# Layer 0's scores in runs of nine over a seven-bank PSUM ring, with exponentials of 1, 1, 3, 2 and 2 banks

## The chip, the cores and the metric

The kernel runs on one NeuronCore of a Trainium2 chip. The metric is the device time of one execution in microseconds, the median of several runs. The profile is one further execution with the hardware profiler on. In the text TensorE (PE) is the matrix engine, with its weight loads shown apart (PEld), ScalarE (ACT) the activation engine, VectorE (DVE) the elementwise engine, POOL the general-purpose engine, SP the engine that only issues DMAs. PSUM, the memory into which TensorE writes[...].

## The reference

Two layers are applied to x (2 images, 256 channels, 64x64 pixels). Layer 0, the only one that the change touches, is a group normalisation, then attention with 8 heads of 32 channels over all 4096 pixels, added to x:

```python
qkv = jnp.einsum('bchw,oc->bohw', x, qkv_w) + qkv_b[None, :, None, None]
...
attn_logits = jnp.einsum('bhci,bhcj->bhij', q, k) * scale
attn_weights = jax.nn.softmax(attn_logits, axis=-1)
out = jnp.einsum('bhij,bhcj->bhci', attn_weights, v)
```

Layer 1 (1x1 convolutions, two attentions within small groups of pixels, a 3x3 convolution) works on the result, and the kernel computes it after layer 0 for each image in turn.

## The kernel before

For each of the two images the kernel makes queries, keys and values (`project0`), then runs layer 0's attention (`attention0`, from L464), then layer 1.

**The tiling of the attention.** The queries of a head are cut into 2 groups of 4 tiles of 512, so an image has 16 groups (g), and the keys into 32 blocks (j) of 128. A *unit* is one key block against one query tile: its score matmul (L505) takes 128 keys as weights (128x128) and 512 queries as the moving data, and fills one PSUM bank. ScalarE takes the exponential of one to three banks with one instruction (L511), without subtracting a maximum, and writes it to `es` in SBUF. A block of four units is then multiplied with its values (`quarters`, L521): the weights are 128x32, the four query tiles lie side by side in the array's four column quarters, and everything of a group adds up in one further bank, `av`. These are fp32 matmuls, each of which the trace shows as two. `work_of` (L570) cuts a block into two halves of 256 columns, save the first and last block of a group; such a half, 8 matmuls in the trace, is a *step*. A group has 62 steps, an image 992.

**The sum of the exponentials** (the softmax's denominator) is made by VectorE (`add_rows`, L558), which adds blocks up elementwise in `added`, and for seven of the 32 blocks by DMAs from POOL's queue that accumulate in SBUF (L566, L568). Once a group is over, `finish` (L592) lets TensorE add the 128 partitions up with a matrix of ones (`sum_rows`), ScalarE copies the result (L598), and after some DMAs and a reciprocal VectorE scales the group's output. The row sum needs a PSUM bank for a short while.

**The rounds.** Seven PSUM banks hold scores, as three tiles: `sa` of three banks, `sb` and `sc` of two. `scores` (L491) fills the three in turn and puts one exponential behind each: a round of seven units. The exponentials go to a ring of 28 places in SBUF (`RING`, L452; 17 in `es`, 11 elsewhere, so `at_places` cuts a group there); `places` holds the place of each unit. In a round in which a row sum (or a small matmul for layer 1's statistics) is due, `sa` takes two units only, and its third bank is lent out (`spare`); this happens 15 times an image for row sums and twice for statistics.

**The order of the work** is written by hand for TensorE, ScalarE and VectorE (`tc.manual_schedule`, L771): their instructions are queued in the order in which the code issues them. The loop from L779 issues a round of scores with its exponentials and then steps of the work on older units: those whose exponentials were issued in earlier rounds (`have`, taken before the round). `share` paces the steps to the units, `must` makes sure that what lies in places about to be overwritten has been used, and a round is broken off where a group ends. What is due with a lent bank stands in `wanted` and is called (`use`) after two steps. The tile framework adds the semaphore waits[...].

The lines that matter below: L500 (the tiles `sa`, `sb`, `sc`), L505 (score matmul), L511 (exponential), L521 (value matmuls and row sums), L598 (copy of a row sum), L762 (copy of a group's `av` bank), L737 (the bank for the last group's row sums), L779 to L804 (the loop).

Of the kernel before, what the change touches and what calls it, by code (L numbers as in the profile page):

```python
# [9 lines left out]
F32 = mybir.dt.float32  # L10
I32 = mybir.dt.int32
F32R = mybir.dt.float32r
AF = mybir.ActivationFunctionType
# [4 lines left out]
P = 128  # L18
B, C, H, W = 2, 256, 64, 64
N = H * W  # L20
T = 512
# [4 lines left out]
NH0 = C // HD0  # L26
# [14 lines left out]
def direct_layers(ctx: ExitStack, tc: tile.TileContext, a: dict, out: bass.AP, bad: bass.AP):  # L41
# [3 lines left out]
    nc = tc.nc  # L45
# [11 lines left out]
    psum = {}  # L57

    def w4(shape, name, dtype=F32):
        return work.tile(shape, dtype, tag="w4", name=name)  # L60
# [304 lines left out]
    SC0 = 1.0 / math.sqrt(HD0)  # L365
# [8 lines left out]
    NJ = N // P  # L374
# [77 lines left out]
    RING, RING_A = 28, 17  # L452
# [11 lines left out]
    def attention0(b, xts, held):  # L464
# [10 lines left out]
        n_units = NH0 * 2 * NJ * 4  # L475
# [4 lines left out]
        places = []  # L480
        n_places = 0

        def at_places(first, n):

            while n > 0:
                at = first % RING
                m = min(n, (RING_A if at < RING_A else RING) - at)
                yield m, es[:, at : at + m, :] if at < RING_A else held["es"][:, at - RING_A : at - RING_A + m, :]
                first, n = first + m, n - m

        def scores(spare):  # L491

            nonlocal n_places
            bank = None
            for tag, size in (("sa", 3), ("sb", 2), ("sc", 2)):
                first = len(places)
                n = min(size - (spare and size == 3), n_units - first)
                if n <= 0:
                    break
                sc = psum["sc"].tile([P, size, T], F32, tag=tag, name=f"{tag}_{b}_{first}")  # L500
                if spare and size == 3:
                    bank = sc[:, size - 1, :]
                for i in range(n):
                    g, (j, u) = (first + i) // (4 * NJ), divmod((first + i) % (4 * NJ), 4)
                    nc.tensor.matmul(  # L505
                        sc[:, i, :], held["k", g // 2][:, j * P : (j + 1) * P], held["q", g, u // 2][:, u % 2, :],
                        start=True, stop=True,
                    )
                i = 0
                for m, dst in at_places(n_places, n):  # L510
                    nc.scalar.activation(dst, sc[:, i : i + m, :], AF.Exp, scale=SC0)  # L511
                    i += m
                places.extend(range(n_places, n_places + n))
                n_places += size
            return bank

        def quarters(dst, lhs, rhs, start, stop, part=None):

# [17 lines left out]
        def add_rows(g, j):  # L536
            if j == 0:
                sums[g] = psum["sc"].tile([P, T], F32, tag="av", name=f"av_{b}_{g}")
                added[g] = [w4([P, 2, T], f"e_{b}_{g}_{w}") for w in range(2)]
                return  # L540
            for w in range(2):
                dst = added[g][w]
                if j in summed(g):
                    if w == 0:
                        add_in_memory(g, j)
                    continue
                if j == 1:
                    first = two_units(g, 0, w), two_units(g, 1, w)
                    if len(first[0]) == len(first[1]) == 1:
                        nc.vector.tensor_add(dst, first[0][0][1], first[1][0][1])  # L550
                    else:
                        for s in range(2):
                            nc.vector.tensor_add(dst[:, s, :], unit(g, 0, 2 * w + s), unit(g, 1, 2 * w + s))
                    continue
                for s, src in two_units(g, j, w):
                    if g == last and j in SUMMED_LAST:
                        continue
                    nc.vector.tensor_add(dst[:, s, :], dst[:, s, :], src)  # L558
# [11 lines left out]
        def work_of(g, j):  # L570


            if (g, j) < (last, NJ - 3):
                add_rows(g, j)
            for part in (None,) if j in (0, NJ - 1) else range(2):
                if part == 1:
                    yield
                quarters(
                    sums[g], held["v"][:, (g // 2) % 2, j, :], lambda u: unit(g, j, u), j == 0, j == NJ - 1, part
                )  # L580

        def sum_rows(g, rows):
            if g == last:
                for part in range(2):
                    for j in SUMMED_LAST:
                        quarters(rows, ones, lambda u: unit(g, j, u), j == SUMMED_LAST[0], False, part)
                    quarters(rows, ones, lambda u: acc[u], False, False, part)
                    quarters(rows, ones, lambda u: added[g][u // 2][:, u % 2, :], False, True, part)
                return
            quarters(rows, ones, lambda u: added[g][u // 2][:, u % 2, :], True, True)  # L590
# [140 lines left out]
        def steps():  # L731

            for done in range(NH0 * 2 * NJ):
                g, j = divmod(done, NJ)
                if (g, j) == (last, NJ - 3):
                    assert len(places) == n_units
                    held["rows"] = psum["sc"].tile([P, 3, T], F32, tag="sa", name=f"rows_{b}")[:, 2, :]  # L737
                    for i in (NJ - 3, NJ - 2, NJ - 1):
                        add_rows(g, i)
                    sum_rows(g, held["rows"])  # L740
                for _ in work_of(g, j):
                    yield done
                if g and j == 0:

                    for w in range(2):
                        dst = added[g - 1][w]
                        for s in range(2) if w == 0 else (slice(0, 2),):
                            nc.vector.tensor_add(dst[:, s, :], dst[:, s, :], acc[s] if w == 0 else pair)
                    waiting.clear()
                if g and j == 1:  # L750
                    wanted.append(late[0].send)
                if g and j in (9, 17):
                    next(late[0])
                for what in also.get((g, j), ()):
                    what()
                if j == 4 and g % 2 == 0 and g // 2 + 1 < NH0:
                    fetch_head(b, g // 2 + 1, held)
                if j == NJ - 1:
                    waiting.append(g)
                    avs = w4([P, 2, T], f"avs_{b}_{g}")  # L760
                    if g < last:
                        nc.scalar.copy(avs[:, 0, :], sums[g])  # L762
                    copied[g] = avs
                    late[:] = [finish(g)]
                    next(late[0])
                    if g + 2 < NH0 * 2:
                        fetch_queries(b, g + 2, held)
                yield done + 1

        E = mybir.EngineType  # L770
        with tc.manual_schedule(engines={E.PE, E.Activation, E.DVE}):  # L771

            per_group = 2 * NJ - 2
            work, begun, taken = steps(), 0, 0
            scores(False)
            final = False
            while not final:  # L779
                have = len(places)  # L780
                use = wanted.pop(0) if wanted else None
                bank = scores(use is not None)
                final = have == n_units
                ready = have // 4
                share = have * per_group // (4 * NJ) - 2

                must = sum(place < n_places + 7 - RING for place in places[: 4 * ready : 4])
                if must % NJ == 1:
                    must += 1
                assert must <= ready  # L790
                here = 0
                while begun < ready and (taken < share or begun < must or final or use is not None):
                    if use is not None and here == 2:
                        use(bank)
                        use = None
                        continue
                    here += 1
                    group = begun // NJ
                    begun = next(work)
                    taken += 1  # L800
                    if begun // NJ > group and begun >= must and not final and use is None:
                        break
                if use is not None:
                    use(bank)  # L804
            assert next(work, None) is None
            return *finish_last(last), st
# [585 lines left out]
    for b in range(B):  # L1392
        xts = x_first if b == 0 else ahead["xts"]
        w0 = w0_first if b == 0 else ahead["w0"]
        with tc.tile_pool(name=f"ps0_{b}", bufs=8, space=PSUM) as psum["ps"]:
# [7 lines left out]
            held = project0(b, xn, w0)  # L1403
# [571 lines left out]
```

## Time and profile before

| what | value |
|---|---|
| time, median of 3 runs | 3115.34 us (3115.27 to 3119.38) |
| span of the profiled execution | 3116.4 us |
| TensorE busy in the span | 3031.2 us (97%) |
| VectorE busy | 2467.0 us (79%) |
| ScalarE busy | 2313.6 us (74%) |
| layer 0's attention, first image | 118 to 1158 us of the span |
| layer 0's attention, second image | 1664 to 2710 us |
| score matmuls (L505) | 4096: 1736 in `sa`, 1180 each in `sb` and `sc` |
| value matmuls into `av` (L521) | 15872 |
| exponentials (L511) | 1770: 590 for each of the three tiles |
| copies of row sums (L598), of `av` (L762) | 30 each, 585 and 607 ns |

The profiled execution's span differs from the median of the runs by 1.1 us. A profile line of the timeline gives the start in us, the length in us, the engine, the line of the kernel, the operation, the tiles written and read, their shapes and the count; in brackets stands the idle time of the engine before it and what ended that. `v` as the output of an exponential is the second part of the ring. The page's slices cut the span into 40 parts and give each engine's busy share in tenths. The granted TensorE clock is 1.00 of full speed throughout the attention.

### The profile page before, as it was taken

How to read it: one execution, taken by the hardware profiler on the slowest of the kernel's cores; microseconds unless marked ns; L12 is line 12 of the kernel's file. 1: busy time of each engine (PE TensorE's matmuls, PEld its weight loads, DVE VectorE, ACT ScalarE, POOL GpSimd, SP SyncE). 2: the span in 40 equal slices, each digit the busy share in tenths (PEclk: the TensorE clock that was granted, in tenths of full speed). 3: DMA queues.
4: the chain of work that ended last, by engine and by line, in shares of the span. 5: the costliest groups of instructions: out<-in, count | busy, mean ns of one | idle time of the engine just before them, and what ended most of it. 6: DMA issues, size and time to landing. Idle time of an engine off the chain costs nothing. (4 is left out here: it accounts for less than half of the span.)

```text
span 3116.4 us, 62659 instructions
## 1 busy us (share of the span) xinstructions
PE 3031.2 (97%) x25129; PEld 1830.6 (59%) x25129; DVE 2467.0 (79%) x3126; ACT 2313.6 (74%) x2436; POOL 836.7 (27%) x923
## 2 busy tenths in 40 slices
PE   6999999999999999999989999999999999999998
PEld 4555555555555556677755555555555555476765
DVE  4599989999899999856556998989989999834543
ACT  2699999999999984622237999999999999734333
POOL 2022222222222231055301222222222222305440
PEclk9999999999999999999999999999999999999999
DMA  7969679797897761230159687796888975700000
GB/s 241 270 132 185 143 150 172 154 178 150 164 181 154 145 133 33 75 134 29 41 193 268 128 176 151 156 176 138 177 162 164 181 153 123 170 4 4 21 14 22
DMA packets 243787, 424.41 MB, mean 136 GB/s; under 512 B 99112, under 2 KB 109916, under 8 KB 241308
## 3 DMA queue, kind: packets, MB, share of 16 engines
q0 software_dynamic: 94992, 238.36, 39.8%
q1 hardware_dynamic: 147580, 181.68, 21.6%
q8 instruction: 199, 3.26, 0.4%
q14 instruction: 104, 0.85, 0.1%
q10 hardware_dynamic: 912, 0.27, 0.0%
HBM read 119.03 MB, written 68.39 MB: 60 GB/s over the span
## 5 line engine op out<-in xcount | busy, mean ns | idle before, releaser
L558 DVE TENSOR_TENSOR e<-e,es 128x1024 f32<-128x1024 f32 (+1 forms) x956 | 1038.6, 1142 | 79.6 <-ACT es L511 77.9
L521 PE MATMUL av<-es,v 128*32 128x256 f32 (+1 forms) x9644 | 746.7, 390 | 0.0
L558 DVE TENSOR_TENSOR e<-e,v 128x1024 f32<-128x1024 f32 (+1 forms) x640 | 675.2, 1107 | 47.7 <-ACT v L511 46.6
L511 ACT ACTIVATE es<-sa 128x1536 f32<-128x1536 f32 (+1 forms) x444 | 635.7, 1432 | 93.1 <-PE sa L505 54.9
L505 PE MATMUL sa<-q,k 128*128 128x512 f32 x1736 | 561.4, 430 | 9.2 <-ACT avs L598 3.5
L521 PE MATMUL av<-v 128*32 128x256 f32 (+1 forms) x6228 | 506.5, 389 | 0.0
L521 PEld LDWEIGHTS av<-es,v 128*32 128x32 f32 x9644 | 316.1, 109 | 299.4 <-issue 160.6
L505 PEld LDWEIGHTS sa<-q,k 128*128 128x128 f32 x1736 | 280.0, 188 | 291.8 <-issue 135.4
L505 PE MATMUL sc<-q,k 128*128 128x512 f32 x1180 | 371.4, 396 | 1.7 <-ACT es L511 0.7
L505 PE MATMUL sb<-q,k 128*128 128x512 f32 x1180 | 371.0, 395 | 1.1 <-ACT es L511 1.1
L521 PEld LDWEIGHTS av<-v 128*32 128x32 f32 x6228 | 216.5, 109 | 178.6 <-issue 81.2
L511 ACT ACTIVATE es<-sc 128x1024 f32<-128x1024 f32 x296 | 306.9, 1037 | 0.0
L511 ACT ACTIVATE v<-sc 128x1024 f32<-128x1024 f32 x294 | 304.9, 1037 | 0.1
L511 ACT ACTIVATE es<-sb 128x1024 f32<-128x1024 f32 x296 | 302.0, 1020 | 3.8 <-DMA acc<-es 3.8
L511 ACT ACTIVATE v<-sb 128x1024 f32<-128x1024 f32 x294 | 300.0, 1020 | 0.0
L505 PEld LDWEIGHTS sb<-q,k 128*128 128x128 f32 x1180 | 221.2, 188 | 55.4 <-ACT es L511 2.9
L505 PEld LDWEIGHTS sc<-q,k 128*128 128x128 f32 x1180 | 210.5, 188 | 71.8 <-ACT es L511 12.1
L511 ACT ACTIVATE v<-sa 128x1536 f32<-128x1536 f32 (+1 forms) x146 | 209.2, 1433 | 35.6 <-PE sa L505 17.0
L948 PE MATMUL mm<-v,wf 128*128 128x256 f32 x1024 | 227.6, 380 | 1.5 <-DVE z L957 1.5
L568 POOL DMA_DIRECT2D es<-es x116 | 98.9, 853 | 475.6 <-ACT es L511 424.3
L948 PEld LDWEIGHTS mm<-v,wf 128*128 128x128 f32 x1024 | 193.3, 190 | 36.8 <-issue 9.9
L938 POOL TENSOR_TENSOR v<-col 128x512 f32<-128x512 f32 x128 | 165.1, 1316 | 179.2 <-ACT rk_sr L1089 39.2
(262 smaller groups left out, 3179.0 us busy)
## 6 DMA issues: line engine op xcount, KB each, us to landing
acc<-es POOLq DMA_DIRECT2D x128, 512.0 KB, 6.2
acc<-v POOLq DMA_DIRECT2D x84, 512.0 KB, 6.4
es<-es POOLq DMA_DIRECT2D x136, 256.0 KB, 4.5
v<-es POOLq DMA_DIRECT2D x132, 256.0 KB, 5.1
k<-wk_halves SPq DMA_DIRECT2D x64, 512.0 KB
q<-wq_halves SPq DMA_DIRECT2D x256, 128.0 KB
v<-v POOLq DMA_DIRECT2D x90, 256.0 KB, 5.4
es<-v POOLq DMA_DIRECT2D x86, 256.0 KB, 3.9
```

The costliest lines, as they stand in the source:

```text
L505: nc.tensor.matmul(sc[:, i, :], held["k", g // 2][:, j * P : (j + 1) * P], held["q", g, u // 2][:, u % 2, :], start=True, stop=True,)
L511: nc.scalar.activation(dst, sc[:, i : i + m, :], AF.Exp, scale=SC0)
L521: nc.tensor.matmul(dst[HD0 * u : HD0 * u + HD0, n], lhs, rhs(u)[:, n], start=start, stop=stop)
L558: nc.vector.tensor_add(dst[:, s, :], dst[:, s, :], src)
L568: nc.gpsimd.dma_start(out=dst, in_=src, accum_op=ALU.add)
L938: (nc.gpsimd.tensor_add if plus else nc.gpsimd.tensor_sub)(dst, rows(one), rows(two))
L948: nc.tensor.matmul(mm[:, m, r, :], wf[:, k, 4 * r + q, m * P : (m + 1) * P], v[r // 2][:, r % 2, k, :], start=k == 0, stop=k == KC - 1,)
```

## The change

The three tiles become one tile of seven banks, `ring`, and a unit's bank is its place modulo 7. A run has nine units, in groups of 1, 1, 3, 2 and 2, each followed by its exponential; `runs_of` cuts a group where it would pass the last bank or the ring's two ends in SBUF. After each score matmul and each exponential, `tc.declare_no_dep` tells the framework that it doesn't depend on the exponentials, or the score matmuls, of the last 21 that use other banks. The lent bank is the next of the ring, and a run that lends one keeps its nine units. In the loop, `have` is taken after the run's scores and reduced by `behind`, 7; `must` looks 10 places ahead instead of 7; a group's last two steps are done in one go (`ending`), and an image's last three blocks wait until all scores are issued.

```diff
--- before.py
+++ after.py
@@ -488,31 +488,53 @@
                 yield m, es[:, at : at + m, :] if at < RING_A else held["es"][:, at - RING_A : at - RING_A + m, :]
                 first, n = first + m, n - m
 
-        def scores(spare):
+        BANKS = 7
+
+        PHASE = (1, 1, 3, 2, 2)
+        recent = {"pe": [], "act": []}
+        ring = psum["sc"].tile([P, BANKS, T], F32, tag="ring", name=f"ring_{b}")
+
+        def spare_bank():
 
             nonlocal n_places
-            bank = None
-            for tag, size in (("sa", 3), ("sb", 2), ("sc", 2)):
-                first = len(places)
-                n = min(size - (spare and size == 3), n_units - first)
-                if n <= 0:
-                    break
-                sc = psum["sc"].tile([P, size, T], F32, tag=tag, name=f"{tag}_{b}_{first}")
-                if spare and size == 3:
-                    bank = sc[:, size - 1, :]
-                for i in range(n):
-                    g, (j, u) = (first + i) // (4 * NJ), divmod((first + i) % (4 * NJ), 4)
-                    nc.tensor.matmul(
-                        sc[:, i, :], held["k", g // 2][:, j * P : (j + 1) * P], held["q", g, u // 2][:, u % 2, :],
-                        start=True, stop=True,
-                    )
-                i = 0
-                for m, dst in at_places(n_places, n):
-                    nc.scalar.activation(dst, sc[:, i : i + m, :], AF.Exp, scale=SC0)
-                    i += m
-                places.extend(range(n_places, n_places + n))
-                n_places += size
-            return bank
+            n_places += 1
+            return ring[:, (n_places - 1) % BANKS, :]
+
+        def runs_of(n):
+
+            at = n_places
+            while n > 0:
+                e = at % RING
+                m = min(n, BANKS - at % BANKS, (RING_A if e < RING_A else RING) - e)
+                yield at, m
+                at, n = at + m, n - m
+
+        def scores():
+
+            nonlocal n_places
+            for size in PHASE:
+                for at, m in list(runs_of(min(size, n_units - len(places)))):
+                    banks = set(range(at % BANKS, at % BANKS + m))
+                    sc = ring[:, at % BANKS : at % BANKS + m, :]
+                    for i in range(m):
+                        unit = len(places) + i
+                        g, (j, u) = unit // (4 * NJ), divmod(unit % (4 * NJ), 4)
+                        made = nc.tensor.matmul(
+                            sc[:, i, :], held["k", g // 2][:, j * P : (j + 1) * P], held["q", g, u // 2][:, u % 2, :],
+                            start=True, stop=True,
+                        )
+                        for past, taken_of in recent["act"]:
+                            if at % BANKS + i not in taken_of:
+                                tc.declare_no_dep(made.ins, past.ins, reason="another bank")
+                        recent["pe"] = (recent["pe"] + [(made, at % BANKS + i)])[-21:]
+                    ((_, dst),) = at_places(at, m)
+                    made = nc.scalar.activation(dst, sc, AF.Exp, scale=SC0)
+                    for past, of in recent["pe"]:
+                        if of not in banks:
+                            tc.declare_no_dep(made.ins, past.ins, reason="another bank")
+                    recent["act"] = (recent["act"] + [(made, banks)])[-21:]
+                    places.extend(range(at, at + m))
+                    n_places = at + m
 
         def quarters(dst, lhs, rhs, start, stop, part=None):
 
@@ -734,7 +756,7 @@
                 g, j = divmod(done, NJ)
                 if (g, j) == (last, NJ - 3):
                     assert len(places) == n_units
-                    held["rows"] = psum["sc"].tile([P, 3, T], F32, tag="sa", name=f"rows_{b}")[:, 2, :]
+                    held["rows"] = spare_bank()
                     for i in (NJ - 3, NJ - 2, NJ - 1):
                         add_rows(g, i)
                     sum_rows(g, held["rows"])
@@ -773,27 +795,32 @@
 
 
             per_group = 2 * NJ - 2
+            behind, reach = 7, sum(PHASE) + 1
             work, begun, taken = steps(), 0, 0
-            scores(False)
-            final = False
-            while not final:
-                have = len(places)
+            while begun < NH0 * 2 * NJ:
+                scores()
                 use = wanted.pop(0) if wanted else None
-                bank = scores(use is not None)
-                final = have == n_units
-                ready = have // 4
+                bank = spare_bank() if use is not None else None
+                final = len(places) == n_units
+                have = n_units if final else len(places) - behind
+                ready = max(0, have) // 4
                 share = have * per_group // (4 * NJ) - 2
 
-                must = sum(place < n_places + 7 - RING for place in places[: 4 * ready : 4])
+                must = sum(place < n_places + reach - RING for place in places[: 4 * ready : 4])
                 if must % NJ == 1:
                     must += 1
                 assert must <= ready
                 here = 0
-                while begun < ready and (taken < share or begun < must or final or use is not None):
+                while begun < ready:
                     if use is not None and here == 2:
                         use(bank)
                         use = None
                         continue
+                    ending = taken % per_group >= per_group - 2
+                    if not (taken < share or ending or begun < must or final or use is not None):
+                        break
+                    if not final and begun == NH0 * 2 * NJ - 3:
+                        break
                     here += 1
                     group = begun // NJ
                     begun = next(work)
```

## The prediction

> **What bounds the kernel now.** I read the page's busy sums and slices first, then the busy time of layer 0's two attention stretches (118 to 1158 us and 1664 to 2710 us, 2086 us together, two thirds of the span), then the instructions of some rounds in order of time.
>
> ```profile
> PE   6999999999999999999989999999999999999998
> ...
> ACT  2699999999999984622237999999999999734333
> ```
> ```profile
> 118.00:1158.00 1040.00, 1034.92 (x10132) 589.17 (x10136) 953.72 (x976) 972.32 (x922) 276.23 (x338) 1.00 0.80 161
> ```
> The line is the first stretch (columns: length, then PE, weight loads, DVE, ACT, POOL busy, TensorE clock, DMA share, GB/s): TensorE is busy 1035 of 1040 us, ScalarE 972, VectorE 954. TensorE bounds, with ScalarE only 6% behind. "Busy" hides gaps inside TensorE, so one round has to be looked at:
>
> ```profile
> 606.18 0.53 PEld L505 LDWEIGHTS sa<-q,k 128*128 128x128 f32 x3 [0.41 <-issue]
> 606.18 0.96 PE L505 MATMUL sa<-q,k 128*128 128x512 f32 x3
> 606.22 1.03 ACT L511 ACTIVATE v<-sc 128x1024 f32<-128x1024 f32 x1
> ...
> 607.18 1.46 ACT L511 ACTIVATE v<-sa 128x1536 f32<-128x1536 f32 x1
> ...
> 607.45 0.63 PE L505 MATMUL sc<-q,k 128*128 128x512 f32 x2
> 608.00 1.02 PEld L521 LDWEIGHTS av<-es,v 128*32 128x32 f32 x24 [0.36 <-issue]
> 608.00 1.50 PE L521 MATMUL av<-es,v 128*32 128x256 f32 x24
> 608.53 1.01 ACT L511 ACTIVATE v<-sb 128x1024 f32<-128x1024 f32 x1
> ...
> 609.43 1.03 ACT L511 ACTIVATE v<-sc 128x1024 f32<-128x1024 f32 x1
> 609.43 0.53 PEld L505 LDWEIGHTS sa<-q,k 128*128 128x128 f32 x3 [0.41 <-issue]
> ```
> Seven scores last from 606.18 to 608.00 (1.82 us), 24 value matmuls from 608.00 to 609.43 (1.43). The next round has 32 value matmuls and takes 1.87 for them (611.25 to 613.12), so a work step of 8 costs 0.43 us and the value part has 1.43 − 3×0.43 = 0.14 us beside its work. Eight 128x32 matmuls of 256 columns, four side by side, stream as many columns as two scores, so a score costs 0.216, seven 1.51, and the score part has 0.31 us beside its work. Each round thus pays **0.45 us** at its two turns between 128x128 and 128x32, where the weight loader sat idle 0.36 and 0.41 us with "issue" as the releaser: not waiting for an engine. ScalarE's starts are 0.90 us apart for two banks (608.53 to 609.43) and 1.35 for three (607.18 to 608.53).
>
> Last, a round with a row sum:
>
> ```profile
> 193.14 1.03 ACT L511 ACTIVATE es<-sa 128x1024 f32<-128x1024 f32 x1 [0.18 <-ACT es L511]
> 193.90 0.59 PEld L521 LDWEIGHTS av<-v 128*32 128x32 f32 x16 [0.36 <-issue]
> ...
> 194.06 1.02 ACT L511 ACTIVATE es<-sb 128x1024 f32<-128x1024 f32 x1
> ...
> 194.79 1.04 PE L521 MATMUL sa<-e,ones 128*32 128x512 f32 x8
> 194.96 1.04 ACT L511 ACTIVATE es<-sc 128x1024 f32<-128x1024 f32 x1
> ```
> The row sum (third bank of `sa`) starts at 194.79, two steps after the scores. The exponential of `sa` has ended at 194.17; those of `sb` and `sc` run until 196.00. It need not wait for them, because they are other tiles.
>
> [...]
>
> **Part 1: fewer turns.** `sb` has 1180 scores, two to a round: 590 rounds in both images. Runs of nine make 2048/9, so 228 an image and 456 in all: 134 fewer. At 0.45 us: **−60 us** of TensorE time, on the path. Scores, value steps and row sums stay as many. The 34 rounds that gave a bank away and held six scores go too; that is in the count.
>
> **Part 2: more activations.** Five groups a run; a group of m is cut again where it crosses bank 6 to 0, or place 17 of the ring of exponentials: (m − 1)×(1/7 + 1/28) on average, 4×5/28 = 0.7 a run. So 5.7×456 = 2600 against 3×590 = 1770. A run costs ScalarE 2×0.485 + 1.35 + 2×0.90 + 0.7×0.06 = 4.16 us. The one-bank form is in no row: [...]I take 0.485. TensorE's run is 9×0.216 + 0.45 + (992 steps/228 = 4.35)×0.43 = 4.26, with row sums 4.32; ScalarE's with its two copies a group (0.6 each, 60 in all) 4.24. TensorE still bounds, by 2% instead of 6%: the additional activations cost nothing by themselves, covered by that 0.08 us a run.
>
> **Part 3: a ring with less slack.** Scores 8 and 9 go to the banks of scores 1 and 2 of the same run. Score 1 at 0; its exponential starts at 0.45 at the earliest (a score alone takes 0.40 us), [...]the ninth score is due at 1.9 and its weight load takes 0.19. [...]The steps come as 4 or 5 a run (a run of 4.11 or 4.54 against 4.24), the copies (0.6 us) make ScalarE late, and where a group ends after few steps TensorE is early. I take 0.05 us a run, **+23 us**; bounds 0 (ScalarE always early) and 0.15 (+68). No gain is possible here, as TensorE had hardly waited for a bank.
>
> **Part 4: the row sum's wait.** Only scores and exponentials are declared independent. The row sum also goes into a bank of the ring, and nothing is declared for it or for its copy. In the compiled program of before, the first row-sum matmul, into bank 2 of `sa`, carries a wait for the exponential that reads banks 0 and 1 of the same tile: dependencies are kept by tile. As the ring is one tile, the row sum must now wait for the last exponential of its run. From score 1 at 0: scores until 2.25, two steps, row sum due at 3.1. Exponentials from 0.45, 4.16 of them, the last one's end 0.12 after its interval: 4.73. Then its weight load: TensorE stands 1.7 to 1.8 us, with the row sum, the run's other two or three steps and the next run queued behind. ScalarE has nothing left meanwhile, so it isn't won back. The copy (0.59) is hidden by those steps, and the next scores wait for it without loss; were there no step left, it would show 0.5 us. This happens 15 times an image, and twice more where statistics borrow a bank: 34 × 1.75 = **+60 us**. Bounds: 0.6 (exponentials nearly done when it comes) and 2.4 (a copy or cut groups before it): 20 to 82.
>
> Edits at nothing: the pacing (`share`) is the same; `behind` 7 is the lag that `have`, taken before the scores, gave; `ending` and the held-back last steps only shift where a run breaks. VectorE's halves follow places that count as before, and its 954 us stay under 1040; if its cover went, ScalarE would wait for a place. POOL's accumulating DMAs are as many and hang on exponentials, not on TensorE; `reach` 10 instead of 7 brings overwriting nearer, and the trace shows 5.6 us of such waits in all. Nothing passes SP or POOL.
>
> **Sum.** −60 + 23 + 60 = +23 us. The profiled execution's span is 3116.4, 1 us over the median 3115.3 and so the same within 0.04%; 3115 + 23 = **3138 us**.
>
> **Rivals.** *A, the forecast:* fewer turns, given back by row sums and a tighter ring. For it: the wait in the program, and `sb` and `sc` unfinished at 194.79. Own range 3122 to 3175. Chance 0.54.
> *B, faster:* the row sum's wait is short, as the dependency doesn't reach beyond its bank or ScalarE is ahead by then. Place: row sum, 34 times; price as above. It decides below (60 − 23)/34 = 1.1 us a wait. At 0.2 us: −60 + 23 + 7 = 3085. Against it: 1.2 us would already have been lost in the round shown, at six scores. Chance 0.28.
> *C, slower by far:* ScalarE becomes the bound. If one-bank exponentials are 0.55 apart, each run gains 0.13 us, and a late ScalarE makes scores 8 and 9 wait: 0.25 us a run in place of 0.05 gives 3138 + 91 = 3229. For it: 2600 activations. Against: it has 5% to spare on average. Chance 0.10.
> *D, nothing much:* turns don't get cheaper with longer runs, or all cancels: 3109 to 3121. Chance 0.08.
>
> Within 0.2% (6 us) is about what a measurement of this kernel can't tell from no change: faster 0.28, same 0.08, slower 0.64. Low end: −60 + 20 + 0 = 3075; high end: −60 + 82 + 68 = 3205, drawn in to 3195. That leaves part of B (0.12) and of C (0.08) outside.
>
> **What would show it.** Step 1: scores' weight loads come in 456 runs with 0.36 to 0.41 us idle. Step 2: about 2600 exponentials, one-bank starts 0.47 to 0.52 apart. Step 3: waits of `ring` matmuls for exponentials, some 20 us. Step 4: the row sums' first weight load idle by about 1.7 us, 30 times, released by the exponential. I am wrong if that idle time is under 1 us, or if ScalarE shows no idle time behind the row sums.

## The result and the profile after

| what | before | after |
|---|---|---|
| time, median of 4 runs each | 3116.38 us (3115.27 to 3119.38) | 3133.55 us (3128.89 to 3135.62) |
| after / before | | 1.0054 [1.0039, 1.0068] |
| span of the profiled execution | 3116.4 us | 3133.7 us |
| attention, image 1 and image 2 | 1043.3 and 1043.7 us | 1052.7 and 1048.8 us |
| runs of scores | 590 | 456 |
| exponentials | 1770 | 2596 |

The change costs 17 us, 0.54%; 23 were forecast. The stretches in the table run from the first score to the last value matmul of an image. Together they are 14.5 us longer. The other 2.8 us of the span lie outside the attention, where the work is the same: there the profiled executions of this case range from 1025 to 1034 us, so a few us mean nothing.

The same parts of the page as before, the busy slices:

```profile
PE   6999999999999999999989999999999999899998
...
ACT  2699999999999974632237999999999999734333
```

They show next to nothing: the first stretch is 0.9% longer, and only digits at the ends of the stretches move. The sums of the stretches say more (columns: length, then PE, weight loads, DVE, ACT, POOL busy, TensorE clock, DMA share, GB/s), first the first stretch of before, then both of after:

```profile
118.38:1161.68 1043.30, 1038.59 (x10188) 590.86 (x10188) 956.24 (x978) 972.73 (x921) 276.95 (x339) 1.00 0.80 161
```
```profile
119.89:1172.57 1052.68, 1023.50 (x10188) 607.62 (x10188) 953.86 (x976) 987.61 (x1334) 277.04 (x339) 1.00 0.79 160
1678.63:2727.47 1048.84, 1019.92 (x10188) 606.57 (x10188) 953.82 (x976) 986.84 (x1334) 273.69 (x339) 1.00 0.79 160
```

Before, TensorE was busy 1038.6 of 1043.3 us in the first stretch, so idle for 5. Now it is busy 1023.5, **15 us less** for the same 10188 matmuls, and idle for **29 us**. Both halves of the forecast are visible here: the work became cheaper and a wait was added that is larger. The list of waits names it (idle time before a matmul: engine, tile and line, what ended it, total us, times, longest):

```profile
PE ring L543 <- ACT es L531: 24.9, 16, 1.7
PE ring L543 <- ACT v L531: 22.8, 15, 2.3
PE ring L318 <- ACT v L531: 3.3, 2, 1.7
PE ring L328 <- ACT v L531: 3.1, 2, 1.6
```

L543 into `ring` is the row sum, L318 and L328 are the two statistics of each image; `es` and `v` are the two parts of the ring of exponentials, so all of these wait for an exponential (L531). The sum is 54.1 us. "Idle" starts at the modelled end of the last value matmul, 0.38 us after its start in the round below, so it is shorter than the delay. From the start of the last value matmul to that of the row sum it is 0.20 us before and 2.02 on average after: the 30 row sums come 1.83 us late (1.68 to 2.48) and, by the same comparison, the four statistics 1.64 to 1.74, 61.5 us in all or 1.81 each.

One round with a row sum, in order of time, answers to the round shown of before:

```profile
259.00 1.91 PEld L522 LDWEIGHTS ring<-q,k 128*128 128x128 f32 x9 [0.41 <-ACT v L531]
259.00 2.33 PE L522 MATMUL ring<-q,k 128*128 128x512 f32 x9
259.54 4.26 ACT L531 ACTIVATE es<-ring 128x512 f32<-128x512 f32 x5 [0.56 <-PE ring L522]
261.26 0.59 PEld L543 LDWEIGHTS av<-v 128*32 128x32 f32 x16 [0.35 <-issue]
261.26 1.07 PE L543 MATMUL av<-v 128*32 128x256 f32 x16
...
263.85 0.16 PEld L543 LDWEIGHTS ring<-e,ones 128*32 128x32 f32 x8 [2.00 <-ACT es L531]
263.85 1.07 PE L543 MATMUL ring<-e,ones 128*32 128x512 f32 x8 [1.52 <-ACT es L531]
...
264.98 0.58 ACT L620 COPY avs<-ring 128x512 f32<-128x512 f32 x1 [1.19 <-PE ring L543]
```

Nine scores from 259.00 to 261.26, two steps until 262.33, and then TensorE stands until 263.85: the five exponentials that began at 259.54 last until 263.80. Only then does the row sum start, 0.05 us after the last exponential's end, though its own bank was never in their hands. ScalarE is idle in turn, 1.19 us before the copy, and 1.11 us more before the next run's first exponential:

```profile
266.68 3.41 ACT L531 ACTIVATE es<-ring 128x512 f32<-128x512 f32 x5 [1.11 <-PE ring L522]
```

So the time isn't won back on the other engine. ScalarE's own work (columns: instructions, then busy us in all and mean ns of one, then idle us before them):

```profile
L531 ACT ACTIVATE es<-ring 128x512 f32<-128x512 f32 (+2 forms) x1572 | 1204.3, 905 | 34.8 <-PE ring L522 28.1
L531 ACT ACTIVATE v<-ring 128x512 f32<-128x512 f32 (+2 forms) x1024 | 781.3, 902 | 33.7 <-PE ring L522 29.6
```

2596 exponentials in place of 1770 add only 15 us a stretch to its busy time (973 to 987), with 65 us of the first stretch left over.

### The profile page after: what moved, and what is told of

It reads as the page before. It is cut to its first block, busy times and chain, and to the rows that moved or that the text cites. A ratio compares the mean times of both kernels' runs of the same rounds, so it can differ in the third digit from the quotient of the medians.

```text
span 3133.7 us, 63967 instructions
## 1 busy us (share of the span) xinstructions
PE 3000.3 (96%) x25129; PEld 1864.8 (60%) x25129; DVE 2459.8 (78%) x3122; ACT 2343.5 (75%) x3262; POOL 836.2 (27%) x923
## 5 line engine op out<-in xcount | busy, mean ns | idle before, releaser
L531 ACT ACTIVATE es<-ring 128x512 f32<-128x512 f32 (+2 forms) x1572 | 1204.3, 905 | 34.8 <-PE ring L522 28.1
L522 PE MATMUL ring<-q,k 128*128 128x512 f32 x4096 | 1081.9, 407 | 4.1 <-ACT es L531 1.9
L522 PEld LDWEIGHTS ring<-q,k 128*128 128x128 f32 x4096 | 733.5, 188 | 373.9 <-ACT es L531 115.6
L531 ACT ACTIVATE v<-ring 128x512 f32<-128x512 f32 (+2 forms) x1024 | 781.3, 902 | 33.7 <-PE ring L522 29.6
L543 PE MATMUL av<-es,v 128*32 128x256 f32 (+1 forms) x9684 | 726.6, 390 | 0.0
L543 PE MATMUL av<-v 128*32 128x256 f32 (+1 forms) x6188 | 496.9, 388 | 0.0
L543 PEld LDWEIGHTS av<-es,v 128*32 128x32 f32 x9684 | 328.2, 110 | 267.3 <-issue 108.4
L543 PEld LDWEIGHTS av<-v 128*32 128x32 f32 x6188 | 220.7, 109 | 170.8 <-issue 72.4
L590 POOL DMA_DIRECT2D acc<-es x118 | 116.5, 987 | 114.2 <-ACT es L531 56.3
L590 POOL DMA_DIRECT2D es<-v x72 | 61.3, 852 | 316.7 <-ACT v L531 306.1
L981 DVE TENSOR_TENSOR z<-z,mm 128x512 f32<-128x512 f32 x32 | 22.0, 686 | 141.4 <-ACT z L980 141.0
L590 POOL DMA_DIRECT2D v<-es x112 | 114.9, 1026 | 24.3 <-ACT es L531 11.6
L590 POOL DMA_DIRECT2D acc<-v x78 | 77.1, 988 | 69.3 <-DMA acc<-es 23.9
L961 POOL TENSOR_TENSOR col<-xp 128x1152 f32<-128x1152 f32 x32 | 69.3, 2165 | 64.3 <-DVE xp L1394 53.0
```

Source lines behind the costliest of these rows:

```text
L522: made = nc.tensor.matmul(sc[:, i, :], held["k", g // 2][:, j * P : (j + 1) * P], held["q", g, u // 2][:, u % 2, :], start=True, stop=True,)
L531: made = nc.scalar.activation(dst, sc, AF.Exp, scale=SC0)
L543: nc.tensor.matmul(dst[HD0 * u : HD0 * u + HD0, n], lhs, rhs(u)[:, n], start=start, stop=stop)
L590: nc.gpsimd.dma_start(out=dst, in_=src, accum_op=ALU.add)
L961: (nc.gpsimd.tensor_add if plus else nc.gpsimd.tensor_sub)(col, cols(one), cols(two))
L981: nc.vector.tensor_add(z[:, 0], z[:, 1], mm[:, :, 0, :])
```

## The experiments

My theory: the turns saved, less what the tighter ring costs, are worth about 47 us, and the undeclared wait of the lent bank takes 61 back. Rivals: the longer runs themselves are dear (the row sum's wait only shows a delay that the next scores would meet anyway), or the many small exponentials are what costs. All runs but one are timed against the kernel before, and the ratios are against it; differences between experiments are of medians.

**Declare the lent bank too.** Each row-sum and statistics matmul, and the copy behind it, is declared independent of recent instructions on other banks, in the manner of the change itself. The lists of recent instructions hold 40 in place of 21; nothing else differs.

```diff
+        def lent_pe(made):
+            if lent[0] is not None:
+                for past, taken_of in recent["act"]:
+                    if lent[0] not in taken_of:
+                        tc.declare_no_dep(made.ins, past.ins, reason="another bank")
+                recent["pe"] = (recent["pe"] + [(made, lent[0])])[-40:]
...
-                nc.tensor.matmul(dst[HD0 * u : HD0 * u + HD0, n], lhs, rhs(u)[:, n], start=start, stop=stop)
+                made = nc.tensor.matmul(dst[HD0 * u : HD0 * u + HD0, n], lhs, rhs(u)[:, n], start=start, stop=stop)
+                if lhs is ones:
+                    lent_pe(made)
...
-            nc.scalar.copy(avs[:, 1, :], rows)
+            lent_act(avs[:, 1, :], rows)
```

(`lent_act` does the same for the copy against matmuls; `lent[0]` is the lent bank's number while `use` runs.)

> The changed kernel with the lent bank declared independent too: the row sums and the two statistics matmuls, and the copies out of their bank, no longer depend on score matmuls and exponentials of other banks. The changed kernel has 34 such matmul groups, each idle for 1.80 us before it (61 us in all). Theory (the idle time is pure loss): 3133 - 61 = 3072 us, faster than the kernel before by about 43; the idle time before the row sums is under 0.2 us. Rival (ScalarE's backlog takes its place, so the wait only moves to the next run's scores): 3110 to 3125, with the waits of score matmuls for exponentials up by 40 us or more.

Measured: 3074.69 us (3071.68 to 3077.07), ratio **0.9858** [0.9842, 0.9875]; 59 us below after, 42 below before. The same kind of round in its timeline (the helper's line is now 560):

```profile
257.09 3.29 ACT L531 ACTIVATE es<-ring 128x1536 f32<-128x1536 f32 x3
...
257.87 1.07 PE L560 MATMUL av<-v 128*32 128x256 f32 x16
...
258.76 1.04 PE L560 MATMUL ring<-e,ones 128*32 128x512 f32 x8
```

The row sum follows the two steps without a break while ScalarE goes on with the run's exponentials until 260.38. The stretches are

```profile
118.69:1142.34 1023.65, 1019.47 (x10188) 609.07 (x10188) 950.13 (x976) 985.37 (x1334) 277.27 (x339) 1.00 0.81 164
1645.50:2671.63 1026.13, 1020.19 (x10188) 607.47 (x10188) 950.78 (x976) 985.26 (x1334) 273.80 (x339) 1.00 0.81 163
```

with TensorE about as busy as after (1019 and 1020 us) and 4 to 6 us of idle time in place of 29. Of the 59 us, 52 lie in the attention, the rest outside it. The 61 us of waits are gone, and about 10 come back: the score parts (from a run's first score to the next value matmul) take 1057.0 us in all against 1052.2, and before two runs TensorE now stands for 2.5 and 2.8 us. The list of waits of scores for exponentials has

```profile
PE ring L522 <- ACT v L531: 5.6, 4, 2.8
PE ring L522 <- ACT es L531: 3.2, 5, 1.8
```

which is far from the 40 us of the rival. So the wait alone makes the change slower. The rest of the change is worth 42 us, 37 of them within the attention.

**Move the row sum.** It is issued after four steps, or at once, in place of two; the wait itself stays.

```diff
-                    if use is not None and here == 2:
+                    if use is not None and here == 4:
```

> The changed kernel with the row sum called after four steps of its run instead of two; its wait for all exponentials of the run stays. The two steps moved ahead of it (0.86 us) fill part of the 1.80 us. Theory of the prediction (the row sum starts when the last exponential ends, at 4.85 us after the first score, wherever it is called; behind it come now no or one step instead of two or three, so the copy out of its bank, which the next scores wait for, is no longer hidden): TensorE's idle time before row sums falls to about 0.95 us, some 0.3 to 0.5 us of it come back as a wait of the next scores for the copy; 34 x 0.3 to 0.5 us gained, 3116 to 3124 us. Rival (the copy costs nothing): 34 x 0.86 = 29 us gained, 3104 us.

Measured: 3112.5 us, ratio 0.9985 [0.9978, 0.9991], 3.5 us under the expected span and 8.5 over the rival's value; 21 us below after, 0.62 a row sum for 0.86 of steps pulled ahead. The missing part has moved, as this kernel's list of waits shows:

```profile
PE ring L522 <- ACT avs L620: 14.6, 30, 0.8
PE ring L543 <- ACT es L531: 11.0, 16, 0.8
PE ring L543 <- ACT v L531: 10.4, 15, 0.9
```

By the starts of the matmuls the waits have halved, from 61.5 to 30.9 us, and the next run's scores, with few or no steps left between, now wait for the copy (L620) of the lent bank, 0.5 us each, 14.6 in all. The two make 16 us less, where the attention is 18 shorter. This was the price that the forecast had named for a copy without cover.

> The changed kernel with the row sum called at once after its run's scores, ahead of all steps. Theory: the wait grows by the two steps that stood ahead of it, 1.80 + 0.86 = 2.66 us, 34 x 0.86 = +29 us: 3162 us. Rival (the wait isn't on the path, since ScalarE sets the pace): no change, 3133 us.

(The same line with `here == 0`.) Measured: 3177.48 us, ratio 1.0185 [1.0168, 1.0202]: 44 us above after, where 29 were expected.

```profile
PE ring L543 <- ACT es L531: 40.9, 16, 2.7
PE ring L543 <- ACT v L531: 34.7, 15, 2.8
```

These and the statistics come to 86 us of idle time against 54, so 32 of the 44. The rest is time in which TensorE is busy: 2057 us in the two stretches against 2043 after, for the same matmuls. After some of these pauses its clock falls. Three windows of this kernel (columns as above; the clock is the third number from the end) and the row sum in them:

```profile
325.00:329.00 4.00, 2.23 (x9) 1.48 (x9) 4.00 (x6) 3.93 (x7) 0.00 (x0) 1.00 0.28 115
329.00:333.00 4.00, 3.21 (x28) 1.21 (x32) 2.88 (x4) 1.32 (x2) 1.77 (x2) 0.57 0.42 71
333.00:337.00 4.00, 4.00 (x45) 2.40 (x41) 0.56 (x1) 2.17 (x4) 0.79 (x1) 1.00 0.42 72
```
```profile
329.79 1.94 PE L543 MATMUL ring<-e,ones 128*32 128x512 f32 x8 [2.56 <-ACT v L531]
```

Eight row-sum matmuls take 1.94 us here and 1.07 after. Such halved stretches, of 3.4 us (one of 6.8), follow 16 of the 34 waits. The attention has four of them after, and one before, at its very start (122.5 to 126.0 us; the clock of 1.00 given for before is rounded). That the remaining 12 us are theirs fits the 14 us more of busy time, but no run isolates it.

**The size and the shape of the runs.** With the lent bank declared too (as in the first experiment), only `PHASE` is changed, so that these are read against 3074.69.

```diff
-        PHASE = (1, 1, 3, 2, 2)
+        PHASE = (1, 1, 3, 2)
```

> As e1_apart, but runs of seven (exponentials of 1, 1, 3 and 2 banks), so that no bank is used twice in a run: 586 runs instead of 456. Theory (each turn pair of the array costs 0.39 to 0.45 us, and longer runs save just that): 130 x 0.39 to 0.45 = +51 to +58 us over e1_apart, 3123 to 3130 us if that is at 3072. Rival ([...]a tighter ring with nine takes most of it back): within 15 us of e1_apart.

Measured: 3103.15 us, ratio 0.9951 [0.9934, 0.9967]; 28.5 above. Both theories were off. Seven scores make 586 runs, 130 more, and 130 × 0.39 (derived below) is +51. Against that stand the waits of the nines for their banks: the time of the score parts above the shortest of its kind is 33.5 us in all with nines and 9.7 with sevens, −24. Of what two more scores a run save in turns, half goes into the tighter ring.

> As e1_apart (3075 us), but runs of eight (exponentials of 1, 3, 2 and 2 banks), so that only one score of a run goes to a bank of its own run: 512 runs instead of 456. Theory (a turn pair costs 0.36 us; the nine's tight ring costs it about 24 us, of which eight have a third or less): 3075 + 56 x 0.36 - 16 to -24 = 3071 to 3079 us. Rival (the tight ring costs nothing that a shorter run saves): 3095 us.

(`PHASE = (1, 3, 2, 2)`.) Measured: 3086.11 us, ratio 0.9896 [0.9883, 0.9909]; 11 above, between the theory and its rival. Eight lie between seven and nine: there are 56 more turns (+22), and the score parts are 15 us above their shortest in place of 33.5, −19. That gives +3, so some 8 us of the 11 aren't accounted for.

> As e1_apart, but runs of eleven with exponentials of 1, 1, 1, 1, 3, 2 and 2 banks: 374 runs instead of 456. Theory: 82 turn pairs less at 0.36 us are 30 us saved, but the eleventh score waits for the fourth exponential of its run, which ends at 2.5 us and lets the score start at 2.75 where 2.36 would be due: 0.39 us x 374 = +146. In all 3190 us. Rival (longer runs go on to pay, as ScalarE keeps up): 3045 us.

(`PHASE = (1, 1, 1, 1, 3, 2, 2)`.) Measured: 3178.81 us, ratio 1.0192 [1.0175, 1.0209]; 104 above. Now four scores go to banks of the same run. The score part's median is 3.087 us, where eleven scores without a wait would take 11 × 0.225 + 0.25 = 2.72: 0.36 × 374 runs = +135, less 82 turns × 0.39 = −32, is +103. Of the lengths run, 7, 8, 9 and 11, nine is the best for seven banks.

> As e1_apart (3075 us), but the first exponential takes two banks: groups of 2, 3, 2 and 2, fewer activations in all. Theory (scores 8 and 9 wait for the exponential of banks 1 and 2 of their own run): that exponential starts at 0.76 us after the first score and ends at 1.8, the eighth score's weight load takes 0.19 more, so it starts at 2.04 instead of 1.66; 0.38 us a run, 456 runs: +173 us, 3230 to 3250 us. Rival (it is ScalarE's work that is tight, so fewer activations help): 3075 or less.

(`PHASE = (2, 3, 2, 2)`: nine scores, but both early ones in one exponential.) Measured: 3157.13 us, ratio 1.0123 [1.0106, 1.014]; 82 above, so half of what the theory asked for, and far from the rival.

```profile
607.11 2.59 PE L522 MATMUL ring<-q,k 128*128 128x512 f32 x9
...
607.88 3.29 ACT L531 ACTIVATE es<-ring 128x1024 f32<-128x1024 f32 x3 [0.61 <-PE ring L522]
...
608.97 0.30 PEld L522 LDWEIGHTS ring<-q,k 128*128 128x128 f32 x2 [0.40 <-ACT es L531]
```

The last two scores are loaded only once the first exponential, of two banks, has ended (it lasts 1.03 us, so until 608.91). The nines' mean is 2.50 us against 2.31 with single first banks: 0.186 × 456 = +85. The expected figure added the whole weight load, 0.19 us, to each wait; in this round the score that follows comes 0.34 us after the one that waited, where 0.23 is usual; the 0.11 more I take for the price of the load. By the code one in seven first groups is cut at the ring's end, which should shorten its wait; this isn't isolated.

> As e1_apart, but nine exponentials of one bank each: 4096 activations instead of about 2600. One-bank activations started 0.475 us apart in the changed kernel, so ScalarE's work grows from about 953 to about 990 us an image, of 1024. Theory (TensorE bounds, and added activations cost only through a later ScalarE at scores 8 and 9): +10 to +30 us, 3085 to 3105 us. Rival (ScalarE sets the pace already in the changed kernel): +37 us an image, 3149 us.

(`PHASE = (1,) * 9`.) Measured: 3120.16 us, ratio 1.0001 [0.9992, 1.001]; 45 above, between the theory and its rival. With 4096 exponentials of one bank ScalarE is busy 1028 of 1044 us of the first stretch: it is very nearly the bound. It isn't with 2596.

> The kernel before's rounds of seven (groups of 3, 2 and 2) in the ring with all banks declared independent, lent bank too. Against e4_apart_7 (3103 us) only the number of activations is smaller, by about a quarter. Theory (added activations cost nothing while ScalarE has slack): within 6 us of e4_apart_7, 3097 to 3109 us, and so still faster than the kernel before, whose rounds with a lent bank held six scores. Rival (each added activation costs its start, 0.05 us, on the path): 25 us less than e4_apart_7, 3078 us.

(`PHASE = (3, 2, 2)`.) Measured: 3111.05 us, ratio 0.9973 [0.9961, 0.9984]; 8 above (1, 1, 3, 2), 2 beyond the expected range, though that kernel has 498 more exponentials. More exponentials are no cost here; that to begin with one bank is a small gain, as the first can start two scores earlier, is likely but not shown. Against before, whose rounds have the same form, this kernel is 6 us faster. So of the 42 us that the best version gains, 6 come with the ring and its declarations, 8 with the form of the groups and 28 with the longer runs.

**Take the declarations out.** The change without its two calls of `declare_no_dep`, run once.

```diff
-                                tc.declare_no_dep(made.ins, past.ins, reason="another bank")
+                                pass
...
-                            tc.declare_no_dep(made.ins, past.ins, reason="another bank")
+                            pass
```

> The changed kernel without its declarations: the ring is one tile in which everything depends on everything. Theory: a group's scores wait for the exponential of the group before, and that for its scores, so about 5.7 groups a run follow one another at 0.7 us for the scores and 0.6 to 1.5 for the exponential: some 10 us a run instead of 4.5, 5500 to 6000 us in all. Rival (the tracking goes by bank, and the declarations change nothing but the row sums): 3130 us.

Measured: 6916.57 us.

```profile
609.36 0.50 PE L522 MATMUL ring<-q,k 128*128 128x512 f32 x1 [0.69 <-ACT es L531]
609.90 0.60 ACT L531 ACTIVATE es<-ring 128x512 f32<-128x512 f32 x1 [0.59 <-PE ring L522]
...
610.55 0.97 PE L522 MATMUL ring<-q,k 128*128 128x512 f32 x3 [0.69 <-ACT es L531]
...
611.61 1.45 ACT L531 ACTIVATE es<-ring 128x1536 f32<-128x1536 f32 x1 [1.10 <-PE ring L522]
```

One group of scores, its exponential, the next group: each waits for the one before, in whatever bank it is. More was lost than expected. The mean granted clock of the execution is 0.698, where after has 0.990; how much of the loss is due to that isn't isolated. So in this program a dependency that isn't declared away reached over the whole tile, at 6916.57 us against 3133.55 with the declarations; the row sum's wait is a remainder of this that the change left in place.

## Why the prediction held

The outcome fell to rival A, the forecast (3138 against 3133.55), with its two opposed terms. By its steps:

**Part 1, fewer turns: right in kind, a little too large.** 134 fewer runs were counted and are there. But a turn was priced at 0.45 us and is worth 0.39. The working had taken a score for 0.216, half of eight 128x32 matmuls. That doesn't follow: eight times 256 columns, four side by side (in the round shown of after four value matmuls start within 0.02 us, and fours 0.22 us apart), are 512 columns, as many as one score has and not two, so it was luck that the figure came near. The medians of the score parts of seven, eight and nine (1.822 before, 2.044 in the runs of eight, 2.272 after) give 0.225 a score and 0.25 beside them, and 0.14 in the value part stands. So −52 and not −60. All that a turn costs beside its work comes to this price here; no run shows what it is made of.

**Part 2, more activations: right.** 2596 exponentials were counted against 2600 forecast. One-bank starts lie 0.477 us apart at the median (nine in ten 0.474 to 0.495), within 0.47 to 0.52 and under the 0.485 taken; two banks 0.90, three 1.33. The 0.485, like the 0.06 for a cut, was the author's estimate: the 1770 exponentials of before are all of two or three banks. One of one bank lasts 0.64 us at the median, and its successor starts 0.16 before its end. ScalarE is idle for 62 to 65 us of each stretch, and the declared lent bank gives the 42 us with the same exponentials. Rival C, ScalarE as the bound, is near only with singles throughout (busy 1028 of 1044 us).

**Part 3, a tighter ring: the cost is there, but part of it was paid before.** The 0.05 us a run was the author's estimate, and how late ScalarE may be at scores 8 and 9 before TensorE waits was not shown. 24 us between sevens and nines in the same ring is what was forecast (23), and the score parts of after lie 23 us above their shortest. Wrong was the base, "TensorE had hardly waited for a bank": the score parts of before already lay 22 us above their shortest, or about 8 above their medians. How much of that was waiting for a bank isn't isolated. The net of the change follows from the sums. Score parts took 1080.4 us before and 1052.2 after, −28.2; the 134 turns of the value side, at 0.14, are −18.8. Together −47.0, of which −52 are turns, so the ring's net is about **+5** in place of +23.

**Part 4, the row sum's wait: right in place, number and size.** 34 times, forecast 1.75, measured 1.81: +61.5 for +60. The lent bank was the one use of the ring in the loop for which the change declared nothing; that a compiled wait of before covered other banks of one tile was the sign, and the undeclared kernel shows such waits before both groups of scores in its timeline above, 0.69 us each. Rival B, a wait below 1.1 us, is wrong for this kernel but near the mark on what the wait is worth: it gave 3085 for 0.2 us a row sum, and with none it is 3074.69.

The sum: −28.2 − 18.8 + 61.5 = +14.5 us, as much as the two stretches grew. The forecast's +23 is 8.5 over that, and 6 over the measured 17. A turn term 8 too large in gain and a ring term 18 too large in cost partly cancel, and 3 us outside the attention, in no term, bring it closer still. So that the total came so close is partly luck.

## What to carry to other kernels

When several buffers are merged into one and their parts are then declared independent by hand, list every instruction that touches it, also the rare borrowers: here 34 undeclared waits of 1.8 us took back more than 134 saved turns gave. Here the steps issued behind the row sum stood too (in the round shown of after it starts at 263.85 us, the next step at 264.73), and the wait was paid almost in full (52 of 61 us in the attention). Price it by how long after it is due its releaser ends, times its count. The best version of those run is the change with the lent bank declared too: 3074.69 us, 1.4% under before.

## What the hardware showed beside this

In the kernel with the row sum called at once, the granted TensorE clock fell to half after 16 of the 34 pauses; in the windows shown for that run it was 0.57 from 329 to 333 us, behind a pause of 2.56 us. The 16 pauses had lasted 2.5 to 2.7 us, and the other 18, after which the clock stayed, 2.5 to 2.9, so in this run their length doesn't tell them apart. No run shows what does.

In the attention of after the clock was 0.50 four times, for 3.41 us each (from 848.25, 1121.31, 1138.38 and 2694.86 us), and in that of before once (from 122.55 us). The mean granted clock of the profiled execution was 0.993 before, 0.990 after, 0.993 with the lent bank declared, 0.984 with the row sum called at once, and 0.698 in the undeclared kernel, where the groups of scores at 609.36, 610.55 and 613.11 us came behind pauses of 0.69, 0.69 and 1.59 us.
